# One mask matmul and one exponential per row half for the second key tile of the local layers

## Chip, cores and metric

The kernel runs on one core of one Trainium2 chip. The metric is the device time of one execution in microseconds (us); of several executions the median is given.

## The reference, cut to what matters

The reference is a network of sixteen blocks on 4096 tokens of width 128 in float32: different attentions, mixtures of experts and feed-forward blocks, each added to its input. The block that matters here is `_L0_ffn_ref`. It is called twice, and each call runs two layers, so a local layer is computed four times. Here it sees 16 sequences of 256 tokens.

```python
DEPTH, HEADS, DIM_HEAD, WINDOW = 2, 8, 64, 64
...
def local_attention(q, k, v):          # q, k l2-normalised, scaled, rotated
    ...                                # each window of 64 queries sees its own and the previous 64 keys
    sim = jnp.einsum('bhwid,bhwjd->bhwij', bq, bk)
    mask = (i < j) | (i > j + WINDOW) | (j == -1)
    sim = jnp.where(mask, -jnp.finfo(sim.dtype).max, sim)
    attn = jax.nn.softmax(sim, axis=-1)
    out = jnp.einsum('bhwij,bhwjd->bhwid', attn, bv)
...
for l in range(DEPTH):
    x = _layer(x, ...)                 # shift, qkv, local_attention, wo, layer norm, gated feed-forward
```

A query sees itself and the 64 tokens before it.

## The kernel before, in words

`local_layer` runs `local_attend` and then `local_ffn`. Activations lie with their 128 features on the partitions and the tokens along the columns; 4096 tokens are 32 tiles of 128 (`NTILE`) and 8 chunks of 512 (`NCH`).

`local_attend` is a software pipeline whose order is written out by hand: under `manual_schedule` every engine runs its instructions in the order in which the program issues them. The loop at L3546 counts slots `m`; 32 of them score. One scoring slot is one sequence and four of the eight heads (`divmod(m, 2)` gives sequence `b` and head group `hg`). The parts of a slot, in their order, with the tile that they work for:

1. `score(m)`: the scores of slot m, transposed, keys on the partitions. Four PSUM banks `ps[0]` to `ps[3]` are taken from the four banks named "s". Heads come in pairs: `a` is the row half (partitions 0 to 63 or 64 to 127 of `qkt` hold the two heads of a pair), `i` counts the two pairs. The first key tile (`t = 0`) is seen by queries 0 to 191, the second (`t = 1`) by queries 128 to 255: blocks of 192 and of 128 columns. In a bank of 512 columns, `ps[a]` holds both 192-column blocks of row half `a` in columns 0 to 383 and the block (i=0, t=1) in columns 384 to 511; `ps[2 + a]` holds the block (i=1, t=1) in columns 0 to 127. The mask of the 192-column blocks is applied by VectorE, which writes `min(score, see)` to `pt` (L3458). The mask of the 128-column blocks is added by TensorE: before the products, a bf16 matmul of the identity `identb` with `masked` (0 or about -1e20) writes it to the place of each block, four matmuls of 128 columns (L3441), and the product accumulates on it. ScalarE then takes the exponentials of the blocks in `ps[2]` and `ps[3]` into `pu` (L3463).
2. `weigh(m - 1)`: the slot before is multiplied with its values `val` into the bank `po` (the one bank "o"); last come the "ones" matmuls, which sum the weights into `pd`. `pd` is the second half, columns 256 to 511, of `ps[3]` of slot m (`spare[3][:, T:]`).
3. `out(c)` in every fourth slot (eight float32 matmul passes and an addition on VectorE).
4. `turn(m + 2)`: eight transposes of a later tile's rotated q and k, two ScalarE copies to `qkt`, the value matmul and its ScalarE copy to `v`.
5. `first_weights(m)`: ScalarE takes the exponentials of the blocks in columns 384 to 511 of `ps[0]` and `ps[1]` into `pu`, and then one of 768 columns in `pt`.
6. `rotate(m + 4)`, `inverse(m - 1)` (ScalarE: logarithm of `pd` into `rd`, then the exponential of its negative), `divide(m - 1)` (VectorE: `ot`), `unit(m + 4)` (ScalarE: two small ones on `ss`, then GpSimd), `chunk_steps(m)` (layer norm and token shift by chunks).
7. `project(m + 5)`: two projections of 512 columns into banks "w" (three banks), their squares `sq` on ScalarE, then four multiplications `t` on VectorE.

The profile gives nearly all ScalarE and VectorE instructions to the helpers `act` (L528), `tt` (L531), `gt` (L534, GpSimd) and `mm` (L504), so instructions are told apart by their tiles: `pu`, `pt`, `rd`, `ss`, `sq`, `v`, `qkt`.

Of the kernel before, what the change touches and what calls it, by code (L numbers as in the profile page):

```python
# [13 lines left out]
AF = mybir.ActivationFunctionType  # L14
# [3 lines left out]
P = 128  # L18
B, T, C = 16, 256, 128
# [1630 lines left out]
class Fast(Net):  # L1650
# [1707 lines left out]
    def local_attend(self, w, z, hs, last):  # L3358
# [6 lines left out]
        with ExitStack() as st:  # L3365
# [10 lines left out]
            masked = one([P, P], "masked", BF16)  # L3376
            self.ts(masked, w["see"][:, :P], 0.0, ALU.min)
            identb = one([P, P], "identb", BF16)
# [3 lines left out]
            made, rot, qkt, val, weights, sums, outs, steps, spare = {}, {}, {}, {}, {}, {}, {}, {}, []  # L3382
# [52 lines left out]
            def score(m):  # L3435


                b, hg = divmod(m, 2)
                qt, kt = qkt[b][:, 0], qkt[b][:, 1]
                ps = [self.bank("s") for _ in range(4)]  # L3440
                for x in (*(b[:, 384:] for b in ps[:2]), *(b[:, :P] for b in ps[2:])):  # L3441
                    self.mm(x, identb, masked, stop=False)

                def product(a, i, t, out):
                    rows, g = slice(64 * a, 64 * a + 64), 2 * hg + i
                    wide = 192 - 64 * t
                    nc.tensor.matmul(
                        out, kt[rows, g, t * P : t * P + P], qt[rows, g, t * P : t * P + wide],
                        start=False, stop=True, skip_group_check=t == 0,
                    )  # L3450

                for i, t, bank, at in ((0, 0, 0, 0), (1, 0, 0, 192), (0, 1, 0, 384), (1, 1, 2, 0)):
                    for a in range(2):
                        product(a, i, t, ps[bank + a][:, at : at + 192 - 64 * t])
                pt = p.tile([P, 2, 384], F32, tag="pt", name="pt", bufs=2)
                pu = p.tile([P, 4, P], F32, tag="pu", name="pu", bufs=2)
                for a in range(2):
                    self.tt(  # L3458
                        pt[:, a].rearrange("p (i t) -> p i t", i=2), ps[a][:, :384].rearrange("p (i t) -> p i t", i=2),
                        self.twice(w["see"]), ALU.min,  # L3460
                    )
                for a in range(2):
                    self.act(pu[:, 2 + a], ps[2 + a][:, :P], AF.Exp)  # L3463
                weights[m] = pt, pu
                spare[:] = ps

            def first_weights(m):
                pt, pu = weights[m]
                for a in range(2):
                    self.act(pu[:, a], spare[a][:, 384:], AF.Exp)  # L3470
                flat = pt.rearrange("p a t -> p (a t)")
                self.act(flat, flat, AF.Exp)

# [70 lines left out]
            with self.share(w=3, s=4, o=1), self.tc.manual_schedule():  # L3544
                self.logs()
                for m in range(-9, NTILE + 6):  # L3546
                    if within(m, NTILE):
                        score(m)
                    if within(m - 1, NTILE):
                        weigh(m - 1)  # L3550
                    c, rest = divmod(m - 5, 4)
                    if rest == 0 and 0 <= c < NCH:
                        out(c)
                    if within(m + 2, NTILE):
                        turn(m + 2)
                    if within(m, NTILE):
                        first_weights(m)
                    if within(m + 4, NTILE):
                        rotate(m + 4)
                    if within(m - 1, NTILE):  # L3560
                        inverse(m - 1)
                        divide(m - 1)
                    if within(m + 4, NTILE):
                        unit(m + 4)
                    chunk_steps(m)
                    if within(m + 5, NTILE):
                        project(m + 5)
# [278 lines left out]
```

## Time and profile before

| | us |
|---|---|
| three runs: median (lowest to highest) | 4256.13 (4253.08 to 4257.88) |
| the profiled execution: its time | 4251.58 |
| the profiled execution: span from first to last instruction | 4249.8 |
| busy: TensorE, VectorE, ScalarE, GpSimd | 3860.8, 2557.6, 2327.2, 1852.0 |
| mean granted TensorE clock | 0.953 |
| the four attention parts of local layers, from the first mask matmul on, end of the last slots included | about 278, 264, 277 and 266 |

The profile names TensorE's matmuls PE and its weight loads PEld, VectorE DVE, ScalarE ACT, GpSimd POOL. A line of the timeline has the start in us from the span's begin, the time from the first start to the last end of the merged group, engine, source line, operation, tiles written and read, shape, and the number of instructions; brackets hold the idle time of the engine before it and what ended it. A float32 matmul appears as two passes per matmul, so eight products are sixteen records. The ends of matmuls are modelled; their starts are better to go by. The 128 scoring slots (four layers of 32) are told apart by their first mask matmul.

### The profile page before, as it was taken

The page shows a single profiled execution, that of the slowest core. Times are in us where ns is not written, and L with a number is a line of the kernel's source. Part 1 is how long each engine was busy: PE and PEld are TensorE (multiplying, and loading weights), DVE is VectorE, ACT ScalarE, POOL GpSimd, SP SyncE. Part 2 cuts the span into 40 slices and gives each one's busy share as a digit, 9 for nine tenths or more (in the row PEclk, how much of TensorE's full clock was granted, in tenths as well). Part 3 has the DMA queues.
Part 4 walks back from the last instruction along what each step waited for, and adds up shares of the span by engine and source line. Part 5 has one row for each costly group of instructions (what it writes and reads, how often), then busy time and mean ns, then how long its engine had stood idle before and what let it go on. Part 6 is the DMA issues. An engine that isn't in the chain of part 4 may idle for free. (4 is left out here: it accounts for less than half of the span.)

```text
span 4249.8 us, 73853 instructions
## 1 busy us (share of the span) xinstructions
PE 3860.8 (91%) x28998; PEld 2207.7 (52%) x28998; DVE 2557.6 (60%) x4503; ACT 2327.2 (55%) x4741; POOL 1852.0 (44%) x1632
## 2 busy tenths in 40 slices
PE   7999999998899999995989979888999999899878
PEld 3555466464465456553965459643444344455333
DVE  4775577364477477555336643565788687486474
ACT  6665466554766456553447634444555455774432
POOL 4664365232565166316433334454555455311251
PEclk9999999988999999997999979999999999999989
DMA  1800000000000000002930049100000000000000
GB/s 61 343 1 1 11 1 1 20 1 1 20 1 1 1 4 2 1 1 83 330 125 12 17 137 316 61 19 16 1 1 1 3 1 1 16 2 18 6 0 21
DMA packets 78404, 176.43 MB, mean 42 GB/s; under 512 B 12606, under 2 KB 39108, under 8 KB 77920
## 3 DMA queue, kind: packets, MB, share of 16 engines
q1 hardware_dynamic: 65568, 148.40, 10.1%
q0 software_dynamic: 9120, 18.51, 1.2%
q8 instruction: 231, 3.78, 0.4%
q10 hardware_dynamic: 3360, 4.72, 0.3%
q14 instruction: 125, 1.02, 0.1%
HBM read 118.28 MB, written 54.20 MB: 41 GB/s over the span
## 5 line engine op out<-in xcount | busy, mean ns | idle before, releaser
L528 ACT ACTIVATE pt<-ps 128x512 f32<-128x512 f32 x640 | 340.0, 600 | 327.7 <-PE ps L504 326.4
L504 PE MATMUL ps<-hb,w 128*128 128x512 f32 (+1 forms) x960 | 458.7, 611 | 6.9 <-issue 3.3
L504 PE MATMUL ps<-w,hb 128*128 128x512 f32 (+2 forms) x896 | 403.4, 571 | 27.9 <-DVE t L531 20.9
L534 POOL TENSOR_TENSOR t<-t,t 128x512 f32<-128x512 f32 x256 | 319.3, 1268 | 160.8 <-DVE t L531 101.2
L531 DVE TENSOR_TENSOR t<-ps,tab 128x512 f32<-128x512 f32 x512 | 317.5, 681 | 83.8 <-ACT sq L528 80.3
L534 POOL TENSOR_TENSOR t<-t,ss 128x1024 f32<-128x1024 f32 x128 | 243.5, 1903 | 218.9 <-ACT ss L528 217.6
L504 PEld LDWEIGHTS ps<-hb,w 128*128 128x128 f32 (+1 forms) x960 | 178.0, 190 | 263.7 <-issue 224.3
L528 ACT ACTIVATE qkt<-ps 128x512 f32<-128x512 f32 x256 | 140.5, 595 | 309.0 <-PE ps L508 308.4
L531 DVE TENSOR_TENSOR u<-u,ps 128x384 f32<-128x384 f32 (+1 forms) x206 | 121.8, 595 | 287.9 <-PE ps L508 182.9
L531 DVE TENSOR_TENSOR ot<-ps,rd 128x512 f32<-128x512 f32 (+2 forms) x224 | 143.2, 639 | 232.0 <-ACT rd L528 232.0
L534 POOL TENSOR_TENSOR nsq<-ha 128x512 f32<-128x512 f32 x112 | 122.9, 1097 | 320.4 <-ACT ha L528 308.6
L504 PEld LDWEIGHTS ps<-w,hb 128*128 128x128 f32 x896 | 155.5, 192 | 185.4 <-issue 113.6
L534 POOL TENSOR_TENSOR both<-pt 128x1024 f32<-128x1024 f32 x64 | 151.2, 2362 | 200.0 <-DVE pt L531 164.3
L504 PE MATMUL ps<-nsq,ct 128*128 128x512 f32 x368 | 201.0, 629 | 36.0 <-POOL nsq L534 32.1
L504 PE MATMUL ps<-ot,w 128*128 128x512 f32 x448 | 213.6, 611 | 16.8 <-DVE ot L531 9.0
L504 PE MATMUL ps<-xt,w 128*128 128x128 f32 x1704 | 221.0, 280 | 1.5 <-ACT xt L528 1.5
L2199 POOL DMA_INDIRECT back<-y,x x142 | 138.9, 978 | 184.2 <-ACT y L528 90.4
L504 PE MATMUL ps<-u,w 128*128 128x512 f32 (+1 forms) x448 | 215.4, 605 | 3.4 <-POOL u L534 3.4
L528 ACT ACTIVATE u<-ps,w 128x512 f32<-128x512 f32 x160 | 107.8, 685 | 183.8 <-PE ps L504 181.3
L504 PEld LDWEIGHTS ps<-xt,w 128*128 128x128 f32 x1704 | 204.8, 194 | 2.9 <-ACT xt L528 2.9
L528 ACT ACTIVATE nrs<-ps,ct 128x512 f32<-128x512 f32 x208 | 139.8, 683 | 101.8 <-PE ps L504 95.9
L3743 POOL DMA_INDIRECT rows<-out,idx x128 | 125.8, 982 | 155.1 <-ACT out L528 105.7
(362 smaller groups left out, 8937.9 us busy)
## 6 DMA issues: line engine op xcount, KB each, us to landing
w<-in_moe_x SPq DMA_DIRECT2D x142, 533.0 KB
rows<-t SPq DMA_DIRECT2D x64, 520.0 KB
x<-rows SPq DMA_DIRECT2D x142, 65.0 KB
w<-in_local_f SPq DMA_DIRECT2D x8, 659.5 KB
y<-back ACTq DMA_DIRECT2D x16, 256.0 KB
y<-back SPq DMA_DIRECT2D x16, 256.0 KB
w<-in_local_f SPq DMA_DIRECT2D x4, 658.5 KB
back<-y,x POOLq DMA_INDIRECT x142
```

What stands on the lines that cost most here:

```text
L504: self.nc.tensor.matmul(out, lhsT, rhs, start=start, stop=stop)
L528: self.nc.scalar.activation(out, in_, func, **kw)
L531: self.nc.vector.tensor_tensor(out, a, b, op)
L534: self.nc.gpsimd.tensor_tensor(out, a, b, op)
L2199: nc.gpsimd.indirect_dma_start(views[i], bass.IndirectOffsetOnAxis(ap=x[:, C : C + 1].bitcast(I32), axis=0), y, None, bounds_check=2 * NT ...
L3743: nc.gpsimd.indirect_dma_start(views[(c * 2 + k) * 4 + t], bass.IndirectOffsetOnAxis(ap=idx[:, k, t : t + 1], axis=0), out[:, k, t], None,)
```

## The change

Both 128-column blocks of a row half, (i=0, t=1) and (i=1, t=1), now lie side by side in columns 0 to 255 of `ps[2 + a]`; columns 384 to 511 of `ps[a]` are no longer used. One mask matmul of 256 columns per row half (the mask read twice by a broadcast) takes the place of two of 128, and one exponential of 256 columns in `score` takes the place of one in `score` and one in `first_weights`. The start and stop flags of the products follow: the first product of `ps[a]` now starts its bank itself, since no mask matmul does.

```diff
                 ps = [self.bank("s") for _ in range(4)]
-                for x in (*(b[:, 384:] for b in ps[:2]), *(b[:, :P] for b in ps[2:])):
-                    self.mm(x, identb, masked, stop=False)
+                for bank in ps[2:]:
+                    self.mm(self.bt(bank[:, :T]), identb, self.twice(masked), stop=False)
 
                 def product(a, i, t, out):
                     ...
                     nc.tensor.matmul(
                         out, kt[rows, g, t * P : t * P + P], qt[rows, g, t * P : t * P + wide],
-                        start=False, stop=True, skip_group_check=t == 0,
+                        start=(i, t) == (0, 0), stop=i == 1, skip_group_check=t == 0,
                     )
 
-                for i, t, bank, at in ((0, 0, 0, 0), (1, 0, 0, 192), (0, 1, 0, 384), (1, 1, 2, 0)):
+                for i, t, bank, at in ((0, 0, 0, 0), (1, 0, 0, 192), (0, 1, 2, 0), (1, 1, 2, P)):
                     for a in range(2):
                         product(a, i, t, ps[bank + a][:, at : at + 192 - 64 * t])
 ...
                 for a in range(2):
-                    self.act(pu[:, 2 + a], ps[2 + a][:, :P], AF.Exp)
+                    self.act(pu[:, a::2], self.bt(ps[2 + a][:, :T]), AF.Exp)
                 weights[m] = pt, pu
                 spare[:] = ps
 
             def first_weights(m):
-                pt, pu = weights[m]
-                for a in range(2):
-                    self.act(pu[:, a], spare[a][:, 384:], AF.Exp)
+                pt = weights[m][0]
                 flat = pt.rearrange("p a t -> p (a t)")
                 self.act(flat, flat, AF.Exp)
```

`bt` splits a row into two halves, `twice` reads one row twice.

## The prediction

> **What bounds the kernel now.** I read the page first, then one group of four scoring slots by windows, then the timelines of PE and ACT inside it.
>
> ```profile
> PE 3860.8 (91%) x28998; PEld 2207.7 (52%) x28998; DVE 2557.6 (60%) x4503; ACT 2327.2 (55%) x4741; POOL 1852.0 (44%) x1632
> ```
>
> ```profile
> core 0: us, PE busy (x) PEld busy (x) DVE busy (x) ACT busy (x) POOL busy (x), PEclk, DMA share, GB/s
> 596.77:604.12 7.35, 7.29 (x84) 4.71 (x83) 5.81 (x9) 5.46 (x15) 4.39 (x3) 1.00 0.00 0
> 604.12:614.96 10.84, 10.70 (x92) 6.29 (x91) 8.23 (x11) 5.07 (x15) 4.39 (x3) 1.00 0.01 2
> 614.96:623.38 8.42, 8.28 (x85) 5.08 (x84) 5.85 (x9) 6.50 (x19) 5.66 (x6) 1.00 0.01 2
> 623.38:631.12 7.74, 7.74 (x85) 5.12 (x84) 5.40 (x9) 5.55 (x17) 6.64 (x7) 1.00 0.01 2
> ```
>
> Each row is one slot: length, then busy time. I call them A, B, C, D. TensorE is busy nearly throughout; no other engine comes near, and DMA does nothing. So ACT time is worth something only where PE waits for it. Those waits hardly show as idle PE, because modelled ends overlap the next start; they show in the starts. B and A:
>
> ```profile
> 604.12 0.69 PE L504 MATMUL ps<-masked,identb 128*128 128x128 bf16 x4
> 604.74 1.37 PE L3447 MATMUL ps<-qkt 64*128 64x192 f32 x16
> ...
> 596.77 0.39 PE L504 MATMUL ps<-masked,identb 128*128 128x128 bf16 x4
> 597.09 1.36 PE L3447 MATMUL ps<-qkt 64*128 64x192 f32 x16
> ...
> 599.28 0.40 PE L3487 MATMUL ps<-pu,v 128*32 128x128 f32 x8
> 599.74 0.53 PE L3487 MATMUL ps<-pt,ct 128*32 128x192 f32 x8
> ```
>
> From mask to product PE needs 0.32 us in A and 0.62 in B: a stall of 0.30. In A the ones matmuls start 0.46 after the last value group; in B the same step takes 0.22, so A stalls 0.24. ACT, from B's preparation on, tells why:
>
> ```profile
> 602.60 0.60 ACT L528 ACTIVATE v<-ps 128x512 f32<-128x512 f32 x1 [0.40 <-PE ps L504]
> 603.10 0.44 ACT L528 ACTIVATE pu<-ps 128x128 f32<-128x128 f32 x2
> 603.41 0.85 ACT L528 ACTIVATE pt<-pt 128x768 f32<-128x768 f32 x1
> 604.14 0.40 ACT L528 ACTIVATE rd<-ps 128x256 f32<-128x256 f32 x1
> 604.57 0.42 ACT L528 ACTIVATE rd<-rd 128x256 f32<-128x256 f32 x1
> 604.89 0.45 ACT L528 ACTIVATE ss<-ss 128x16 f32<-128x16 f32 x2
> 605.25 1.07 ACT L528 ACTIVATE sq<-ps 128x512 f32<-128x512 f32 x2
> 606.20 0.45 ACT L528 ACTIVATE pu<-ps 128x128 f32<-128x128 f32 x2
> ```
>
> From the copy of v, which waits for PE, ACT runs without a gap to the next slot's `pu`. The logarithm of `pd` (604.14 to 604.54) frees `ps[3]`; the fourth mask matmul, 604.59, waits for it. In A the last pair of `pu` ends at 599.69 and the ones matmuls, which write the same bank, follow at 599.74. Third, VectorE's `t` starts when the first square ends (598.90 in A) and its fourth frees a "w" bank at 601.39, 0.05 before the value matmul: about 0.19 of stall. All three hang on this ACT chain.
>
> **The Trainium skill.** *TensorE: Matmul & The Clock Gate*, section "Back-to-back issue gap", gives N/2.4 + 2.5 ns between single matmuls: 56 ns at 128 columns, 109 at 256. The trace's masks start 55 to 57 ns apart, which agrees; 256 columns in bf16 are not in the trace. *ScalarE: Activation LUTs*, "Rules for kernel authors", budgets about 0.3 us per ACTIVATE plus 0.83 ns per element. The trace has 0.279 at 128 columns, 0.396 at 256 (`rd<-ps`) and 0.595 at 512: the slope agrees, the fixed part is nearer 0.17, and back to back these overlap, so I use starts. *PSUM — Partial Sum Buffer*, "The four PSUM rules": a first matmul clears the written-bits of its whole bank, and a later one overwrites where they are clear. Hence the flag edit only moves the clearing from mask to product; no run here prices it, and I take zero.
>
> **The change part by part.** Per slot:
>
> *ACT, first_weights.* Two exponentials go: 603.10 to 603.41, so `pt`, logarithm, `ss`, squares each start 0.31 earlier relative to v. `pt` inherits the wait for VectorE's minimum, over by 602.3: no cost.
>
> *ACT, score.* Two exponentials of 256 take the place of two of 128. Starts are 0.155 apart at 128 and 0.48 at 512 (squares), so 0.26 at 256; the pair ends 0.26 + 0.40 = 0.66 after its start instead of 0.45: 0.21 later, but started 0.31 earlier, hence 0.10 earlier relative to v. Behind it stand the `qkt` copies (ACT idles 1.43 there for PE: covered) and the ones matmuls, which wait on it in A and C. Where the pair waits for products instead (D), it ended 0.56 before the ones; 0.21 fits.
>
> *PE masks.* 4 x 0.056 against 2 x 0.109: equal streaming. Before, 0.09 of the next weight load stays exposed after the last mask; a longer mask may hide it. I take 0.01 per slot (1 us); bounds 0 and 0.09 (12 us), and a loss of 0.1 per mask if the doubled read streamed at half rate (27 us over 256 masks), which no row here suggests.
>
> *Waits moved.* Banks are handed out in the order they come free. In the built program a steady slot's `ps[2]` needs no new wait; mask 2 and product a=0 wait for VectorE's minima, long over; product a=1 waits for the logarithm. It was mask 4. Behind it PE's whole queue stands, as before, but the logarithm ends at 0.11 after the first mask instead of 0.42 and the product would start at 0.32: the 0.30 goes. DVE, POOL and SP keep their order; no DMA moves.
>
> Per kind of slot, with counts from all 128:
>
> - slots 2 to 6 of each layer, stall at the logarithm only: 20 x 0.30 = 6.0.
> - groups ABCD (34.35 us, 14 of them). A: ones 0.10 earlier, then the 0.19 at v goes too because `t` comes 0.31 earlier: 0.29. B: 0.30. C: its 0.30 at the logarithm only lengthens the wait at the ones, net 0.10, plus 0.18 at v: 0.28. D: nothing. 0.87 x 14 = 12.2.
> - groups of 37.96 us (6, in first layers of a pair, which have norm steps as well): one slot waits 0.90 for the copy of `ha`, which ends this chain: 0.31; one nothing; one ones-bound: 0.10; one held by `t` twice: 0.31. 0.72 x 6 = 4.3.
> - three late slots of each layer, in which little other PE work is left and PE waits long for the logarithm: 12 x 0.31 = 3.7. The earlier stalls at masks 2 and 3 there, behind `pu`, vanish into the same wait. One of these twelve; the bracket is PE's idle time and its releaser:
>
> ```profile
> 733.79 0.22 PE L504 MATMUL ps<-masked,identb 128*128 128x128 bf16 x1 [0.79 <-ACT rd L528]
> ```
>
> Sum 26.2, with masks 27. What is late next is PE itself. Later stages follow in order, so the whole of it should reach the end. Against the profiled execution: 4251.6 - 27 = 4224.6. The median of the runs stands 4.5 above that execution, so the forecast is 4256.1 - 27 = **4229**.
>
> **Rivals.**
> 1. *The pair in score ends no earlier* and VectorE's `t` does not follow: only the pure logarithm stalls go: 6.0 + 14 x 0.30 + 3.7 = 14; 4242. For it: the ones matmuls (PEld at L3487) already wait for `pu` 40 times, as the view of this tile says (us, times). Against: the chain from v has no gap.
>
> ```profile
>   PEld ps L3487: 11.6, 40
> ```
>
> 2. *The mask-to-product load hides as well*, and product a=1 follows the logarithm closer than 0.20 in last slots: 27 + 10 = 37; 4219. Possible, unseen.
> 3. *Slower: the clock.* TensorE is denser by 2.5% in these stretches. The granted clock is 0.953 over the span but 0.99 to 1.00 in the local stretches, so there is something to lose. The local stretches would take 1084 - 27 = 1057 us; 2.6% less clock there eats the 27 us, and from 3.4% on the kernel is slower by more than 0.2%. At 4% it adds 42 us: 4271. Against: runs agree within 5 us, and slot lengths repeat to 0.01.
> 4. *It does not do what it says*: the built instruction streams hold 256 fewer exponentials and 256 fewer mask matmuls, so this is excluded; but as said, the matmuls save no columns.
>
> **How the numbers follow.** Chances: forecast (22 to 32 us) 0.55; rival 1 and between (9 to 22) 0.20; rival 2 0.12; within 0.2% (8.5 us, about what a measurement can tell from no change) 0.06; slower 0.07. The range takes in rivals 1 and 2 and the bound of the masks: 4213 to 4246.
>
> **What would show it.** In the changed profile: 256 `pu` at about 0.40; B's mask-to-product 0.32; the last `pu` before the ones in A ending 0.1 earlier relative to v; the group of four near 33.5 instead of 34.35. Wrong: a group still over 34.1, ones waits grown past 0.4 in A, or masks more than 0.13 apart.

## The result, and the profile after

Four runs of each kernel on one chip: 4217.30 us after (4216.72 to 4217.79) against 4256.45 before (4253.08 to 4257.88). The ratio is 0.9909, 95% interval 0.9897 to 0.9921: **39.2 us saved, where 27 were forecast** (4217 against 4229; the range 4213 to 4246 holds it). The profiled execution of the changed kernel took 4216.97 us, its span 4215.2; between the two profiled executions 34.6 us are gone.

The line of busy times in the page of the kernel after:

```profile
PE 3849.9 (91%) x28742; PEld 2195.1 (52%) x28742; DVE 2557.5 (61%) x4503; ACT 2314.2 (55%) x4485; POOL 1854.9 (44%) x1632
```

256 matmuls and 256 ACT instructions fewer. ACT is busy for 13.0 us less and PE for 10.9; VectorE and GpSimd hardly move. The gain is three times what either was relieved of, so it can't be read here. The windows of a group ABCD in the kernel after, one row a slot (length, then busy time of each engine):

```profile
core 0: us, PE busy (x) PEld busy (x) DVE busy (x) ACT busy (x) POOL busy (x), PEclk, DMA share, GB/s
588.54:595.57 7.03, 7.03 (x82) 4.57 (x80) 5.53 (x9) 5.36 (x12) 4.40 (x3) 1.00 0.02 3
595.57:606.10 10.53, 10.53 (x89) 6.18 (x88) 8.23 (x11) 4.95 (x13) 4.41 (x3) 1.00 0.00 0
606.10:614.22 8.12, 7.95 (x83) 4.95 (x82) 6.14 (x10) 6.35 (x18) 5.66 (x6) 1.00 0.01 2
614.22:621.96 7.74, 7.74 (x83) 5.00 (x82) 5.41 (x10) 5.54 (x15) 6.65 (x7) 1.00 0.01 3
```

33.42 us instead of 34.35. A, B and C are each 0.30 to 0.32 shorter, D is as long as it was. The starts on PE in B and, below, at the ones matmuls of A, from the timeline of the kernel after:

```profile
595.57 0.38 PE L504 MATMUL ps<-masked,identb 128*128 128x256 bf16 x2
595.88 1.36 PE L3447 MATMUL ps<-qkt 64*128 64x192 f32 x16
...
591.04 0.40 PE L3485 MATMUL ps<-pu,v 128*32 128x128 f32 x8
591.38 0.53 PE L3485 MATMUL ps<-pt,ct 128*32 128x192 f32 x8
```

From mask to product B needs 0.31 (0.62 before). In A the ones matmuls start 0.34 after the last value group (0.46 before): half of the stall there is left. ACT from the copy of v on, for slot B:

```profile
594.05 0.60 ACT L528 ACTIVATE v<-ps 128x512 f32<-128x512 f32 x1 [0.21 <-PE ps L504]
594.54 0.83 ACT L528 ACTIVATE pt<-pt 128x768 f32<-128x768 f32 x1
595.28 0.38 ACT L528 ACTIVATE rd<-ps 128x256 f32<-128x256 f32 x1
...
596.36 1.07 ACT L528 ACTIVATE sq<-ps 128x512 f32<-128x512 f32 x2
597.32 0.66 ACT L528 ACTIVATE pu<-ps 128x256 f32<-128x256 f32 x2
```

v to logarithm: 1.23 instead of 1.54. v to the end of `pu`: 3.93 instead of 4.05. So the chain came 0.31 earlier in its middle and 0.12 earlier at its end, where 0.31 and 0.10 were forecast; a pair of 256 columns takes the predicted 0.66 (0.39 for each, starts 0.26 to 0.28 apart).

**Where the 39 us lie.** The four stretches from slot 0 to slot 31 of the local layers sum to 1044.0 us before and 1009.8 after (-34.2); the rest of the span is 3205.8 and 3205.3. The last 4.5 us are the distance from the profiled execution to the median: 4.9 before, 0.3 after. They need not be chance: on another chip the two medians, 4273.11 and 4234.15, lie 39.0 apart again, which is also some 5 us more than the slots give. No run shows where these lie. In the 34.2 there are 4.8 beyond the length of any wait: three short stretches of half clock, which experiment 6 takes up. The other 29.4 agree with the waits of PE, added up over the 128 slots from starts: about 66 us before and 37 after.

### The profile page after: what moved, and what is told of

Same layout as the page of the kernel before. It is cut to its first block, busy times and chain, and to the rows that moved or that the text cites. A ratio compares the mean times of both kernels' runs of the same rounds, so it can differ in the third digit from the quotient of the medians.

```text
span 4215.2 us, 73089 instructions
## 1 busy us (share of the span) xinstructions
PE 3849.9 (91%) x28742; PEld 2195.1 (52%) x28742; DVE 2557.5 (61%) x4503; ACT 2314.2 (55%) x4485; POOL 1854.9 (44%) x1632
```

## The experiments

Each kernel was timed against the kernel before on its own chip; three chips took part, with that kernel at 4254.73, 4277.15 and 4273.11 us. Slot lengths of one kernel agree over the chips to 0.02 us, a layer's first slot and those with half clock apart; the 20 us lie outside the local slots. "Slots" below is the sum over the four stretches, from the profiled execution.

### 1. Layout and masks alone

The new layout with its two masks, but four exponentials of 128 where they stood.

```diff
-                    self.act(pu[:, a::2], self.bt(ps[2 + a][:, :T]), AF.Exp)
+                    self.act(pu[:, 2 + a], ps[2 + a][:, P:T], AF.Exp)
 ...
-                pt = weights[m][0]
+                pt, pu = weights[m]
+                for a in range(2):
+                    self.act(pu[:, a], spare[2 + a][:, :P], AF.Exp)
```

> The changed layout and its two mask matmuls of 256 columns, but four exponentials of 128 where they stood: two in score, two in first_weights. Theory (the gain is the 0.31 us taken out of ACT's chain between v and the logarithm): the group ABCD stays near 34.3 us, B's and C's wait for the logarithm is back (mask to second product 0.6), about 4248 us. Rival (the new order of banks and masks carries the gain): the group is near 33.4 and the time within 8 us of the changed kernel, 4217 to 4225.

Measured: 4238.60 us, ratio 0.9966 (0.9951 to 0.998), between the two expectations. The group takes 34.20, B 10.69 instead of 10.84, a slot of 2 to 4 7.04 instead of 7.19; slots 1031.6. So the layout alone brings 12.4 us of slot time, 4.8 of it the half clock. ACT's order is that of before, and the logarithm still ends 0.42 after the first mask. What changed is who waits: the whole mask work and the product a=0 now run ahead of the wait, and 0.15 of each 0.30 is gone. The prediction put the whole 0.30 down to the exponentials; half of it goes with the move of the wait alone. The two overlap: in experiment 2's second order, with the masks of before and all exponentials early, B takes 10.54, so the whole 0.30 is gone there without the new masks. The remaining 21.8 us of slots come with the exponentials.

### 2. Four early exponentials without the new layout

If only the time of the exponentials matters, the old layout could do with all four in `score`. Two orders were tried: banks 0 and 1 first, and banks 2 and 3 first.

```diff
                 for a in range(2):
+                    self.act(pu[:, a], ps[a][:, 384:], AF.Exp)
+                for a in range(2):
                     self.act(pu[:, 2 + a], ps[2 + a][:, :P], AF.Exp)
 ...
-                pt, pu = weights[m]
-                for a in range(2):
-                    self.act(pu[:, a], spare[a][:, 384:], AF.Exp)
+                pt = weights[m][0]
```

> The layout and four masks of before, four exponentials of 128, but all four in score, bank 3 last. Theory (place, not number, of the exponentials): ACT's chain is 0.31 us shorter up to the squares, but the last exponential of score ends 0.75 instead of 0.66 us after the first starts, so the ones matmuls wait as long as before: group 33.6 to 33.7, about 4224 to 4228 us. Rival (fewer ACT instructions, or the masks, carry the gain): above 4240 us.

Measured: 4688.89 us, ratio 1.1017 (1.0999 to 1.1035). A miss of more than 430 us, with the sign reversed. The view of the tile `pu` in this kernel (us, times) and a line of its ACT timeline:

```profile
its engine sat idle before it (us, times) until:
  DVE pt L531: 363.8, 252
who waited for it (us, times):
...
  PE ps L3487: 322.0, 124
```

```profile
658.54 0.28 ACT L528 ACTIVATE pu<-ps 128x128 f32<-128x128 f32 x1 [2.53 <-DVE pt L531]
```

ACT sat idle for VectorE's minimum, which reads columns 0 to 383 of the same bank; that minimum (657.96) stood behind four `t`. Then the ones matmuls, and all of PE, waited for ACT. Not all of the loss is waiting: the slots of this kernel have 324 us of half clock (experiment 6) against 10 before, and half of the difference, an estimated 157 us, is what that costs. The page *PSUM — Partial Sum Buffer* of the Trainium skill, section "PSUM bank collisions raise a hardware error", gives a reason for such a wait: accesses to PSUM must be kept apart by bank and not by address, reads by two engines included. The trace agrees as far as it goes: the columns are disjoint, and the exponential starts after VectorE is done. That the two reads could not overlap was not tried.

With banks 2 and 3 first:

```diff
                 for a in range(2):
                     self.act(pu[:, 2 + a], ps[2 + a][:, :P], AF.Exp)
+                for a in range(2):
+                    self.act(pu[:, a], ps[a][:, 384:], AF.Exp)
```

> The layout and masks of before, all four exponentials of 128 in score, those of banks 2 and 3 first, so that the ones matmuls wait for none behind VectorE. Theory (in the old layout the early exponentials stand behind VectorE's minimum of the same bank, and hold up ACT's copies of qkt): no ones stall of 2.8 us per slot as with bank 3 last, but ACT 0.5 to 1 us late at the copies: group 34.6 to 36.5, about 10 to 60 us slower than before. Rival (only the ones matmuls' place behind them was costly): faster than before, group 33.5 to 34.0.

Measured: 4285.72 us, ratio 1.0032 (1.002 to 1.0044), group 35.38. ACT still idles 291.6 us for the minimum, 240 times, but the bank that the ones need is read first, and little of the wait for `pu` is left at the ones. What reaches PE comes through the `qkt` copies queued behind it; in the view of PE's waits (us in all, times, longest) the kernel before has no such row:

```profile
PE ps L504 <- ACT qkt L528: 30.7, 55, 0.7
```

In either order the early exponential of banks 0 and 1 costs. So the move of those blocks into a bank that VectorE never reads is what lets their exponential stand in `score` at all. The prediction named no such condition.

### 3. The bank of the ones first

A and C of the kernel after still stall at the ones, which wait for the pair's second exponential because it reads the bank of `pd`. The other order frees that bank 0.26 earlier.

```diff
-                for a in range(2):
+                for a in (1, 0):
                     self.act(pu[:, a::2], self.bt(ps[2 + a][:, :T]), AF.Exp)
```

> The changed kernel with the two exponentials of score in the other order, bank 3 first. Theory (the ones matmuls wait for the exponential that reads bank 3): it ends 0.26 us earlier, the ones stall of A (0.12) goes and that of C (0.35) falls to 0.09: group near 33.05, about 6 us less, 4211 us. Rival (the late ones matmuls are TensorE's own, the releaser a coincidence): unchanged at 4217 us, group 33.43.

Measured: 4218.86 us, ratio 0.9921 (0.9904 to 0.9937), not told apart from 0.9909. The group is 33.37, not 33.05. The waits of PE in the first local layer (us in all, times, longest), this kernel first, then the kernel after:

```profile
PE ps L508 <- DVE t L531: 1.8, 3, 0.6
```

```profile
PE ps L508 <- DVE t L531: 1.0, 3, 0.3
...
PE ps L3485 <- ACT pu L528: 0.9, 5, 0.2
```

The row for `pu` is gone from the first view; the row for `t` has grown by 0.8. Over all slots the ones stall fell from 10.3 to 1.5 us, but the slots fell by 3.0 us alone: the other 5.8 came back at the transposes, the value matmul and the projections, where PE waits for `t`. VectorE's `t`, which hangs on the squares, is late next. The same kernel again:

> Bank 3's exponential first, once more, beside the changed kernel on one chip. The slots are 3.0 us shorter in its first profile. Theory (it reaches the end): 2 to 4 us less than the changed kernel. Rival (lost in the half-clock windows elsewhere): 0 to 2 more.

Measured: 4242.09, ratio 0.993 (0.9918 to 0.9942) beside 0.9903 for the kernel after on that chip: slots again 1006.8, the rest of the span 5.9 longer, with 453 us of low clock in it against 423. Where 2 to 4 us less were expected, the median is 8 more. Three microseconds in the slots don't show in the time.

### 4. Two idle exponentials where the two were

To price the ACT time alone: the changed kernel with two exponentials of 128, from a tile of zeros to one that nobody reads, ahead of `pt`.

```diff
             def first_weights(m):
                 pt = weights[m][0]
+                for a in range(2):
+                    self.act(junk[:, a], none, AF.Exp)
```

> The changed kernel with two exponentials of 128 columns put back into first_weights, from a tile of zeros in SBUF to a tile that nobody reads, so that no bank and no matmul is touched. Theory (ACT time ahead of the logarithm is what counts): the group is back at 34.2 to 34.5 us, and the kernel at 4246 to 4252. Rival (banks and masks): 4217 to 4222 us.

Measured: 4237.63 us, ratio 0.9965 (0.9951 to 0.9979); group 34.42, slots 1038.5. In the slots 28.7 us come back, nearly the 29.4. So ACT time at this place does cost PE time. But what was put back is more than what the change took out, as ACT's timeline of this kernel shows:

```profile
242.71 0.60 ACT L528 ACTIVATE v<-ps 128x512 f32<-128x512 f32 x1 [0.21 <-PE ps L504]
243.20 0.50 ACT L528 ACTIVATE junk<-none 128x128 f32<-128x128 f32 x2
243.60 0.83 ACT L528 ACTIVATE pt<-pt 128x768 f32<-128x768 f32 x1
244.33 0.37 ACT L528 ACTIVATE rd<-ps 128x256 f32<-128x256 f32 x1
```

The idle pair, from SBUF to SBUF, holds `pt` back by 0.40 where the pair from PSUM took 0.31, so the logarithm starts 1.62 after v, against 1.54 before. Nor are the masks of before back, and one slot came out 1.35 short for the reason in experiment 5. The near match of 28.7 and 29.4 is therefore in part chance. The kernel is 6.9 us worse than experiment 1, which has its late exponentials in the same place: the slower idle pair and the longer pair in `score` (256 columns, not 128) both lie in that, and no run separates them. The time lies 8 us under the expected band; of that the slots explain nothing, the rest of the span (3197.4 against 3205.3) all.

### 5. ACT's small work taken off the chain

The squares still have two `ss` instructions ahead of them. In this kernel `unit` leaves the end of the slot and is issued in the next one, right after `weigh`, where ACT idles for PE.

```diff
                     if within(m - 1, NTILE):
                         weigh(m - 1)
+                    if within(m + 3, NTILE):
+                        unit(m + 3)
 ...
-                    if within(m + 4, NTILE):
-                        unit(m + 4)
```

> The changed kernel with unit (two small ScalarE instructions on ss, 0.35 us from start to start, and a GpSimd product) moved from before the squares of its slot to behind score of the next slot. Theory (squares, VectorE's t and the exponentials of score hang on one ACT chain from v): all three start 0.35 us earlier, so the ones stalls (0.12 in A, 0.35 in C) go without t taking their place: group near 32.96 against 33.43, 11 us less in all, 4206 us. Rival (another order only swaps one wait for the next, GpSimd's product comes too late): group 33.4 or longer, 4217 us or more.

Measured: 4214.70 us, ratio 0.9855 (0.9839 to 0.9872), group 32.91, slots 990.2: 19.6 less than the kernel after, where 11 were expected. The difference lies in the groups of norm steps. One slot of theirs, PE's timeline in the kernel after, then here:

```profile
258.35 0.66 PE L508 MATMUL ps<-ct,t 128*128 128x128 f32 x4 [0.33 <-DVE t L531]
259.54 1.13 PE L504 MATMUL ps<-w,hb 128*128 128x512 f32 x2 [0.54 <-DVE t L531]
```

```profile
252.24 1.09 PE L508 MATMUL ps<-ct,t 128*128 128x128 f32 x8
253.17 1.11 PE L504 MATMUL ps<-w,hb 128*128 128x512 f32 x2
```

Both waits for `t` are gone, and the wait for `pu` ahead of them; the slot falls from 9.47 to 7.84. Here the squares are only part of the cause, for `unit` also holds GpSimd's product `t<-t,ss`. In the kernel after it starts just ahead of a VectorE instruction that stands before the four `t`. The two in the kernel after, then the same VectorE instruction here:

```profile
254.64 1.91 POOL L534 TENSOR_TENSOR t<-t,ss 128x1024 f32<-128x1024 f32 x1 [4.05 <-ACT ss L528]
254.79 2.31 DVE L531 TENSOR_TENSOR ha<-ha,nrs 128x512 f32<-128x512 f32 x1
```

```profile
250.02 0.68 DVE L531 TENSOR_TENSOR ha<-ha,nrs 128x512 f32<-128x512 f32 x1
```

So VectorE's instruction takes 1.6 us more when GpSimd's product has begun 0.15 before it; all six of these and the six `hb<-hb,w,nrs` of the norm-step slots show it in the kernel after, none here. One slot of experiment 4's kernel shows that the order of the two starts decides, in otherwise equal code: there VectorE began first, and it was GpSimd's product that took longer.

```profile
257.72 0.68 DVE L531 TENSOR_TENSOR ha<-ha,nrs 128x512 f32<-128x512 f32 x1
257.86 2.30 POOL L534 TENSOR_TENSOR t<-t,ss 128x1024 f32<-128x1024 f32 x1 [4.74 <-ACT ss L528]
```

That slot takes 8.51 instead of 9.86. Six slots at 1.35 each are an estimated 8.1 us, which with the expected 11 come near the 19.6. With bank 3 first as well:

> The same with the exponential of bank 3 first. Theory: the ones stalls are gone already, so at most 1 us less than without it: 4205 us. Rival (the exponentials still end after the ones could start): 3 to 6 us less than without it.

4218.55 us, ratio 0.9862 (0.9845 to 0.9878), slots 990.0: nothing is left to take at the ones. The first version once more, beside the kernel after on one chip:

> unit behind score once more, beside the changed kernel on one chip. The slots are 19.7 us shorter in its first profile than in that of the changed kernel. Theory (TensorE bounds the local layers, all of it reaches the end): 17 to 22 us less than the changed kernel. Rival (half-clock windows elsewhere take it back): less than 8.

> The changed kernel once more, on the chip of the next three runs: every theory expects the ratio to before near 0.991 again and slot lengths as in its first profile to 0.02 us (group 33.43), with no half-clock window in the late slots.

4217.86 us, ratio 0.9869 (0.9855 to 0.9884), against 4234.15 us, ratio 0.9903 (0.9889 to 0.9918): 16.3 us faster than the changed kernel, just under the 17 to 22 expected. This version beats both.

### 6. The short stretches of half clock

Before has three of them in late slots. One such slot in PE's timeline of the kernel before, and the windows row at half clock (second number the length, the number after POOL's the clock):

```profile
386.70 0.39 PE L504 MATMUL ps<-masked,identb 128*128 128x128 bf16 x2 [0.80 <-ACT pu L528]
387.88 0.22 PE L504 MATMUL ps<-masked,identb 128*128 128x128 bf16 x1 [0.79 <-ACT rd L528]
```

```profile
388.90:392.30 3.40, 3.40 (x50) 2.50 (x50) 1.69 (x4) 0.45 (x2) 0.00 (x0) 0.50 0.00 0
```

Slot 29 takes 12.45 us there and 10.84 in a layer without such a stretch. Slots 29 and 30 of every layer wait like this. After has one wait of 0.95 in each of the two and no half clock. If the waits bring it, longer waits in the changed kernel must bring it back: two idle exponentials of 512 ahead of the logarithm, in three slots of each layer.

```diff
             def inverse(m):
 ...
+                if NTILE - 6 <= m < NTILE - 3:
+                    for a in range(2):
+                        self.act(junk[:, a], none, AF.Exp)
```

> The changed kernel with two idle exponentials of 512 columns (zeros in SBUF to a tile that nobody reads) ahead of the logarithm in the three late slots of each layer, which puts 0.96 us more of TensorE's wait into each, so about 1.95 us as before the change. 12 x 0.96 = 11.5 us by itself, 4229 us. Theory A (the long waits brought the half-clock windows that the profile of before has in late slots 29, 94 and 125 and that of the changed kernel has not): two or more such windows of 3.4 us appear in these slots, 1.7 us each. Theory B (where these windows fall is chance): none or one.

> The kernel before, unchanged, for a second profile of it. Theory A: again half-clock windows in the late slots of two or more layers, all slot lengths else as in the first profile to 0.02 us. Theory B: none or one, or elsewhere. Both expect 4253 to 4258 us.

Measured with the waits: 4253.15 us, ratio 0.9945 (0.9928 to 0.9961). One wait, and the stretch that begins as it ends, of that kernel:

```profile
381.88 2.50 PE L3450 MATMUL ps<-qkt 64*128 64x192 f32 x14 [1.99 <-ACT rd L528]
```

```profile
381.60:388.40 6.80, 6.52 (x63) 4.87 (x64) 2.28 (x4) 1.41 (x4) 0.00 (x0) 0.50 0.01 2
```

Half clock is back in three layers of four. Before, run again (4276.26 us, ratio 0.9995, 0.9986 to 1.0003), has two such stretches, in two of the same three slots. So PE's waits bring it, though not every time: five layers of eight with 1.59 us in two pieces, three of four with 1.99 in one. Experiment 2's first order, with 124 waits of 2.6 us on average, has the 324 us named there. The ten profiles without any in their local slots wait less in slots 29 and 30: 0.95 in seven of them, 1.22 in two pieces (experiment 1), 1.35 (experiment 4) and 1.52 (experiment 2, second order). Where between these the limit lies, and whether the place in the slot matters, stays open: 1.52 and 1.59 are too near each other, and four layers too few.

## Why the prediction was right, and where its sizes were off

- **The bound: right.** PE is the bound, and ACT counts where PE waits for it. The ACT chain runs as forecast (0.31 and 0.12 earlier for 0.31 and 0.10), and ACT time put back at that place lengthens the slots again (experiment 4).
- **Per slot, groups ABCD: right.** 0.31, 0.30, 0.30 and 0.00 for 0.29, 0.30, 0.28 and 0: 14 x 0.91 = 12.7 us for 12.2. As forecast, C exchanged its stall at the logarithm for a longer one at the ones: 0.35 there now, 0.17 before. Slots 2 to 6: 20 x 0.31 = 6.2 for 6.0. Groups with norm steps: 0.79 for 0.72, so 4.7 for 4.3.
- **Late slots: mis-sized.** "12 x 0.31" took one gain for all. Measured, slots 28, 29 and 30 lose 0.27, 0.48 and 0.49, in a layer without half clock: 5.0 us for 3.7. The masks and the first product now run ahead of the wait, and two waits became one. The kernel before has a mask and its step to the product behind the logarithm (it ends at 740.93 in the first view, and the product starts 0.19 later). In the kernel after (ACT's line, then PE's) two records of product a=0 are through, and the rest start 0.04 after its end at 384.73:

```profile
740.53 0.40 ACT L528 ACTIVATE rd<-ps 128x256 f32<-128x256 f32 x1
...
741.12 1.36 PE L3447 MATMUL ps<-qkt 64*128 64x192 f32 x16
```

```profile
384.35 0.38 ACT L528 ACTIVATE rd<-ps 128x256 f32<-128x256 f32 x1
```

```profile
382.92 0.38 PE L504 MATMUL ps<-masked,identb 128*128 128x256 bf16 x2
383.23 0.59 PE L3447 MATMUL ps<-qkt 64*128 64x192 f32 x2
384.77 1.36 PE L3447 MATMUL ps<-qkt 64*128 64x192 f32 x14 [0.95 <-ACT rd L528]
```

- **Masks: right.** 256 columns in bf16 are not slower than twice 128, broadcast read or not: mask to product is 0.31 for 0.32. The 0.01 per slot (1 us) can't be told from the rest, and the bound of 0.09 was not reached.
- **The wait moved from mask 4 to product a=1: right, and worth more than "it goes".** Experiment 1 shows that the move alone takes 0.15 of each stall of 0.30, with the logarithm where it was; in late slots it adds to the 0.31.
- **The sum.** These steps give 28.6 us for 27, and the slots show 29.4 without half clock. The rest of the miss was no step at all: 4.8 us of half-clock stretches, which the prediction considered only as a danger (rival 3, with the other sign), and 4.5 because it carried before's distance from profiled execution to median over to the kernel after. So 39.2 lies outside the 22 to 32 to which it gave its best chance, while the part that its steps priced lies inside.
- **Rivals.** Rival 1 falls: the pair does end earlier, and `t` follows. Rival 2's total, 37, came nearest, by luck. The load that it would hide stays: from the last mask to the product it is 0.20 after and 0.146 before, and less the masks' own spacing (0.109 and 0.055) that leaves 0.09 in both. Its second half came true, with 0.04 from logarithm to product in late slots, but is worth the 1.3 us by which those were mis-sized, not the rest of its 10. Rival 3 falls: the clock in the local slots is 1.00 after and lower in three places before.
- **What was not seen.** That the early exponential needs a bank which VectorE doesn't read (experiment 2) would not have changed the number, but it is the condition of the whole change.

Open: what moves the part outside the local slots. It has 380 to 450 us of low clock in these runs and differs by up to 12 us between kernels that are equal there, on one chip, and by 20 between chips. Experiment 3 lost its 3 us in it, experiment 4 seemed to gain 8.

## What to carry to other kernels

Price an instruction on an engine that is not the bound by the starts of the engine that is: here two exponentials of 0.28 us busy time, issued ahead of a wait, cost 0.31, 0.16 and 0.30 us of PE time in slots A, B and C and nothing in D (experiment 1 against the kernel after, the longer pair in `score` included). When work is to move earlier, ask who else reads its buffer: sharing a PSUM bank with another engine's reads turned a gain into a loss of 10%, or of 0.3% in the other order. After a stall goes, look at what is late next (here `t`, behind two small ACT instructions and, in some slots, a VectorE instruction slowed by GpSimd), for that is where the next version comes from.

## What the runs showed of the hardware that was not expected

- The Trainium skill's page *TensorE: Matmul & The Clock Gate*, section "HAM oscillation — how this bites in real kernels", warns of idle gaps on TensorE of more than about 3.4 us. The half-clock stretches here last 3.4 us, or two in a row, 6.8, but the waits that brought them were much shorter: 0.80 and 0.79, or 1.99. The measurement decides: a wait of 0.95 us brought none in seven profiles, and 1.6 to 2.0 us in one slot could cost another 1.6 (12.45 against 10.84).
- A VectorE instruction on two SBUF tiles (`ha<-ha,nrs`, 128x512, f32) took 2.31 us when a GpSimd product had begun 0.15 us before it, and 0.68 when that one began later; GpSimd's then took 2.30 instead of 1.91 (experiment 5).
- Two exponentials of 128 columns hold the next ACT instruction back by 0.31 us when they read PSUM and by 0.40 when they read SBUF (experiment 4).
